# A four-layer convolution sequence: channel mixing on row halves of TensorE, fewer split column transforms, more convolutions put off

## The chip, the cores and the metric

The kernel runs on one core of one Trainium2 chip. The metric is device time in microseconds (us) of one execution. The kernel before takes 2974.68 us, the median of three runs (2972.39 to 2974.85). Engines are named as in the profile: PE is TensorE (PEld its weight loads), DVE is VectorE, ACT is ScalarE, SP is the engine that issues most DMAs.

## The reference, cut to what matters

The input x has 4 images of 64 channels of 256 x 256 float32. Four layers follow one another. Layers 0, 1 and 3 are long convolutions with a separable filter for each channel; layer 2 mixes channels in a Haar transform.

```python
def conv_layer(x, hx, hy, bias):      # layers 0, 1, 3; hx, hy from a small sine network
    k = hx[i, c] * hy[j, c]           # one separable 256 x 256 filter for each channel
    y = irfft2(rfft2(x, 512x512) * rfft2(k, 512x512))[..., :256, :256]
    return y + x * bias[c]            # causal 2D convolution plus a scaled copy

def haar_layer(x, v, conv_w, tau):    # layer 2
    f1 = haar2d(x)
    for i in range(2):
        f4 = einsum('bchw,oc->bohw', f1 * v[i], conv_w[i])
        acc += sign(f4) * relu(abs(f4) - tau[i])
    return haar2d(acc, inverse=True) + x
```

The filter is separable and causal, so a convolution is two products with Toeplitz matrices, one for rows and one for columns. A float32 value enters the matmuls in full precision.

## The kernel before, in words

**Units.** Work goes by image b and channel c. One channel image is a tile of 128 partitions by 2 x 256 (two halves of the rows). A convolution has two stages: `first` contracts the image with the Toeplitz tile of one axis (`contract`, L190 and L191), ACT copies the result out of PSUM (L199); `second` contracts that with the other axis's tile and DVE adds the bias term (L212). A `contract` is two halves m, each of one float32 matmul of 256 columns and one of 128. Toeplitz tiles `t` are read from small padded filters in DRAM (L181).

**`convolutions(b, ...)`** runs layers 0 and 1 on all channels of an image, then the forward Haar transform along the row in three parts: `pairs` (L257, L258), `levels` (L269, L270), and along the column by TensorE in `down`. For a channel in `in_parts`, `split` makes two f32r parts of it: ACT casts it (L280) and DVE subtracts the cast from it (L281). `down` then does two f32r matmuls of 512 columns with the sign matrix (L288). For a channel not in `in_parts`, `down` does a single float32 matmul of 512 columns on the tile itself (L292) and no `split`. Before, all channels of all images are in `in_parts`. ACT copies the coefficients out (L296), and SP stores them to `coef` in DRAM.

**`mixing(b, start, n_act)`** goes over 64 groups g of four coefficient rows. `load` brings a tile `f` in which partitions 0 to 63 hold the 64 channels of two rows and partitions 64 to 127 those of two others (r = 0, 1). `mix` (L335 to L346) multiplies it with `wb`, a block-diagonal matrix of 128 x 256: four matmuls of 256 columns into two PSUM banks. Half of `wb` is zero. Then 16 blocks of 64 values are scaled by v: 16 - `n_act` of them in one DVE instruction (L357), `n_act` by ACT, one instruction each (L359). `shrink` takes magnitude and sign on ACT (L365, L366) and subtracts the threshold on DVE (L367), `signed` multiplies (L372), `add` writes the sum of the two mixings into z in SBUF (L376). `n_act` is 12 for images 0 to 2 and 6 for image 3.

**`inverse(b, start, put_off)`** goes over the 64 channels: `fetch` loads `keep` and copies the channel out of z (L396), `rows` does the inverse transform along the row (L403, L404) and splits the result (L406 on ACT, L407 on DVE), `cols` does the column (L416) and adds the residual (L420, L423, L424). The result u then goes through layer 3 (`last`, two contractions and a store of the output from ACT's queue, L443), except for the channels in `put_off`: their u is stored to `late` in DRAM (L434), also from ACT's queue.

**`convolution(which, ticks)`** does layer 3 later for the channels put off by images 0 to 2: SP loads u back as `v` (L453) and the Toeplitz tile, then `last` follows. Before, every third channel is put off: 21 per image, 63 in all.

**Order of the work.** Each stage is entered with `at(tick, place, run, unit)`, and at the end all events are emitted sorted by tick and place (L500). Each engine and each DMA queue then runs its own instructions in that order. The main loop (L487 to L499) lays them out so: the convolutions of image 0 alone; then for each image b its mixing, beside the convolutions of image b + 1, spread over the mixing's ticks and the inverse stage ahead of it; then its inverse. Beside the mixing of image 3, which has no image after it, the put-off convolutions run. After the end of a mixing (`border`) the last column transforms of the next image are set three ticks apart for each one.

```python
    put_off = range(2, C, 3)
...
        mixing(b, start, 12 if b + 1 < B else 6)
        end = start + groups + 3
        if b + 1 < B:
            ready = convolutions(b + 1, spread(ahead, end + 2), in_parts=range(C), border=end)
```

**Buffers.** Incoming images and `v` share three buffers (tag "in"), Toeplitz tiles five, `f` three, mixing results in PSUM two (of two banks each), results of contractions in PSUM four.

Of the kernel before, what the change touches and what calls it, by code (L numbers as in the profile page):

```python
# [9 lines left out]
F32 = mybir.dt.float32  # L10
# [7 lines left out]
P = 128  # L18
# [19 lines left out]
def conv_seq_kernel(ctx, tc, x, fz, fw, bias, decay, haar, haar_row, factors, vt, taut, wmix, out):  # L38
# [14 lines left out]
    nc = tc.nc  # L53
# [15 lines left out]
    hbr = const.tile([P, P], F32R, name="hbr")  # L69
    hrow = const.tile([P, 2, P], F32, name="hrow")  # L70
    hsinv, ident = hrow[:, 0, :], hrow[:, 1, :]
    wb = const.tile([P, 2, P], F32, name="wb")
    bsb = const.tile([P, 3, C], F32, name="bsb")


    z = zpool.tile([P, 2, S, C], F32, name="z")

    sd = zpool.tile([P, 8, 2, 2, P], F32, name="sd")
    keep = [dram.tile([C, P, 2, 2, P], F32, name=f"keep{b}") for b in range(B)]
# [4 lines left out]

    room = z.rearrange("p h r c -> p (h r c)")
    free = [0]

    def part(n, parts=P):  # L90
# [57 lines left out]
    def constants():  # L148
        signs = part(P)
        nc.sync.dma_start(hbt, haar[0])  # L150
        nc.sync.dma_start(signs, haar[1])
        nc.sync.dma_start(hrow, haar_row)
        nc.vector.memset(wb, 0.0)
        for r in range(2):
            nc.sync.dma_start(wb[r * C : (r + 1) * C, r, :], wmix)
        nc.scalar.copy(hb, signs)
        nc.scalar.copy(hbr, hbt)

# [57 lines left out]

    def butterfly(b):

        d = mx.tile([P, 2, C], F32, name=f"bfly_{b}", tag="mag")
        nc.vector.tensor_sub(d, z[:, :, 0, :], z[:, :, 1, :])  # L220
        nc.vector.tensor_add(z[:, :, 0, :], z[:, :, 0, :], z[:, :, 1, :])
        nc.vector.tensor_copy(z[:, :, 1, :], d)

# [90 lines left out]
    def mixing(b, start, n_act):  # L316

        st = {}

        def load(g):  # L320
            f = mx.tile([P, 2, S], F32, name=f"f_{b}_{g}", tag="f", bufs=3)
            nc.sync.dma_start(f, coef[b].rearrange("k c p w -> (k c) p w")[:, 2 * g : 2 * g + 2])
            st[g] = {"f": f}
            if g % GT == 0:
                t = mx.tile([P, 2, GT, 16], F32, name=f"vt_{b}_{g}", tag="vt")
                nc.sync.dma_start(t, scales[g // GT])
                st["vt", g // GT] = t

        def scale(g, i):
            return st["vt", g // GT][:, i, g % GT, :]  # L330

        def over(g, i, n):
            return scale(g, i)[:, :n].unsqueeze(2).to_broadcast([P, n, C])

        def mix(g):  # L335
            f = st[g]["f"]
            ps = psx.tile([P, 2, 2, S], F32, name=f"px_{b}_{g}", tag="mix")
            for q in range(2):
                for h in range(2):
                    nc.tensor.matmul(  # L340
                        ps[:, h, q, :],
                        f[:, q, h * P : (h + 1) * P],
                        wb.rearrange("p r n -> p (r n)"),
                        start=True,
                        stop=True,
                    )  # L346
            if g == 0:

                one, two = ps[:, :, 0, :P], ps[:, :, 0, P:]
                d = mx.tile([P, 2, P], F32, name=f"d_{b}", tag="mag")  # L350
                nc.vector.tensor_copy(d, two)
                nc.vector.tensor_sub(two, one, d)
                nc.vector.tensor_add(one, one, d)
            f4 = mx.tile([P, 16, C], F32, name=f"f4_{b}_{g}", tag="f4")
            px = ps.rearrange("p h q (r i o) -> p (h q r i) o", r=2, i=2)
            n = 16 - n_act
            nc.vector.tensor_tensor(f4[:, :n], px[:, :n], over(g, 0, n), ALU.mult)  # L357
            for j in range(n, 16):
                nc.scalar.mul(f4[:, j], px[:, j], scale(g, 0)[:, j : j + 1])  # L359
            st[g]["f4"] = f4  # L360

        def shrink(g):
            f4 = st[g]["f4"]
            mag = mx.tile([P, 16, C], F32, name=f"mag_{b}_{g}", tag="mag")
            nc.scalar.activation(mag, f4, AF.Abs)  # L365
            nc.scalar.activation(f4, f4, AF.Sign)  # L366
            nc.vector.tensor_sub(mag, mag, over(g, 1, 16))  # L367
            st[g]["mag"] = mag

        def signed(g):  # L370
            mag = st[g]["mag"]
            nc.vector.scalar_tensor_tensor(mag, mag, 0.0, st[g]["f4"], ALU.max, ALU.mult)  # L372

        def add(g):
            parts = st.pop(g)["mag"].rearrange("p (h r i) o -> p h r i o", h=2, i=2)
            nc.vector.tensor_add(z[:, :, 4 * g : 4 * g + 4, :], parts[:, :, :, 0, :], parts[:, :, :, 1, :])  # L376

        for g in range(S // 4):
            at(start + g - 2, 0, load, g)

            for s, (place, stage) in enumerate([(-2.5, mix), (-3.5, shrink), (-4.1, signed), (-4.2, add)]):
                at(start + g + s, place, stage, g)

    def inverse(b, start, put_off):

        st = {}

        def fetch(c):  # L390
            if c == 0:
                butterfly(b)
            r = mx.tile([P, 2, 2, P], F32, name=f"r_{b}_{c}", tag="f", bufs=3)
            nc.sync.dma_start(r, keep[b][c])
            a = mx.tile([P, 2, 2, P], F32, name=f"zc_{b}_{c}", tag="mag")
            nc.scalar.copy(a, z[:, :, :, c].rearrange("p h (i k) -> p h k i", k=2))  # L396
            st[c] = {"r": r, "z": a}

        def rows(c):
            a = st[c]["z"]  # L400
            ps = psm.tile([P, 2, 2, P], F32, name=f"pw_{b}_{c}", tag="mm")
            for m in range(2):
                nc.tensor.matmul(ps[:, m, 0, :], a[:, 0, m, :], hsinv, start=True, stop=True)  # L403
                nc.tensor.transpose(ps[:, m, 1, :], a[:, 1, m, :], ident)  # L404
            w = mx.tile([P, 2, 2, 2, P], F32R, name=f"w_{b}_{c}", tag="f4")
            nc.scalar.copy(w[:, 0], ps)  # L406
            nc.vector.tensor_tensor(w[:, 1], ps, w[:, 0].bitcast(F32), ALU.subtract)  # L407
            st[c]["w"] = w
            if c not in put_off:
                st[c][2] = toeplitz(2, c, f"t2_{b}_{c}")  # L410

        def cols(c):
            ps = psm.tile([P, 2, 2, P], F32, name=f"pu_{b}_{c}", tag="mm")
            flat = "p m e w -> p (m e w)"
            for i in range(2):
                nc.tensor.matmul(  # L416
                    ps.rearrange(flat), hb, st[c]["w"][:, i].rearrange(flat), start=(i == 0), stop=(i == 1)
                )
            t = io.tile([P, 2, 2, P], F32, name=f"t_{b}_{c}", tag="res", bufs=BUFS["res"])
            nc.vector.scalar_tensor_tensor(t, st[c]["r"], 0.5, ps, ALU.mult, ALU.add)  # L420
            u = io.tile([P, 2, S], F32, name=f"u_{b}_{c}", tag="y", bufs=BUFS["y"])
            v = u.rearrange("p m (w e) -> p m w e", e=2)
            nc.vector.tensor_add(v[:, :, :, 0], t[:, :, 0, :], t[:, :, 1, :])  # L423
            nc.vector.tensor_sub(v[:, :, :, 1], t[:, :, 0, :], t[:, :, 1, :])  # L424
            st[c]["u"] = u

        ends = last(b, st)
        for c in range(C):

            at(start + c, -1, fetch, c)  # L430
            at(start + c + 1, -9, rows, c)
            at(start + c + 2, -8, cols, c)
            if c in put_off:
                at(start + c + 3, -5, lambda c: nc.scalar.dma_start(late[b, c], st.pop(c)["u"]), c)  # L434
            else:
                for s, stage in enumerate(ends):
                    at(start + c + 3 + s, s - 7, stage, c)

    def last(b, st):
        return [  # L440
            first(b, st, "u", 2, "a3"),
            second(b, st, "a3", 2, "u", "y3", "co"),
            lambda c: nc.scalar.dma_start(out[b, c].rearrange("(k p) w -> p k w", p=P), st.pop(c)["y3"]),  # L443
        ]

    def convolution(which, ticks):

        for (b, c), tick in zip(which, ticks):
            st = {}

            def load(c, b=b, st=st):
                u = io.tile([P, 2, S], F32, name=f"v_{b}_{c}", tag="in", bufs=3)
                nc.sync.dma_start(u, late[b, c])  # L453
                st[c] = {"u": u, 2: toeplitz(2, c, f"t2_{b}_{c}")}

            for s, stage in enumerate([load, *last(b, st)]):
                at(tick + s, -s, stage, c)


# [1 line left out]
        return [begin + i * (end - begin - 1) // (n - 1) for i in range(n)]  # L461


    put_off = range(2, C, 3)

    one, two, three = filters(0, nc.scalar), filters(1, nc.scalar), filters(2, nc.sync)

# [17 lines left out]
    ahead = C  # L485
    start = ready + 3
    for b in range(B):  # L487
        mixing(b, start, 12 if b + 1 < B else 6)
        end = start + groups + 3
        if b + 1 < B:  # L490
            ready = convolutions(b + 1, spread(ahead, end + 2), in_parts=range(C), border=end)
        else:
            convolution(
                [(i, c) for i in range(B - 1) for c in sorted(put_off)], spread(start - 2, end + 2, (B - 1) * len(put_off))
# [116 lines left out]
```

## Time and profile before

| What | us |
|---|---|
| Median of 3 runs | 2974.68 |
| The profiled execution | 2975.2 |
| Its span | 2973.4 |
| Matmuls of the mixing (L340), busy | 488.2 |
| Convolutions' matmuls `py<-t,a` (L190), busy | 919.0 |
| DVE threshold L367 and product L372, busy | 312.4 and 311.7 |
| ACT scaling L359, busy | 582.3 |
| ACT casts of the split L280, DVE subtractions L281, busy | 177.6 and 176.1 |
| DMA, mean over the span | 219 GB/s |

The granted TensorE clock is 1.0 throughout. The profile is of one execution; its own time stands 1.8 us above its span. A busy time is the union of an engine's instructions, so instructions that overlap count once. Each engine runs in order, so an instruction that waits holds up all behind it on that engine. The chain of waits gives PE by far the largest share. DVE's busy time is an average over stages with different limits, so each stage has to be looked at alone. Where an f32 matmul is written in the kernel, the trace has two MATMUL and two LDWEIGHTS instructions.

### The profile page before, as it was taken

What the parts mean: (1) busy time and instruction counts of PE and PEld (TensorE: products, weight loads), DVE (VectorE), ACT (ScalarE), POOL (GpSimd) and SP (SyncE); (2) the same over time, 40 slices, a digit from 0 to 9 for tenths busy, and PEclk for the clock granted to TensorE, in tenths of its full rate; (3) what the DMA queues carried; (4) which work ended last, traced back from release to release, by engine and by line L of the source; (5) the groups of instructions that cost most, each with busy time, mean ns of one, the idle gap of its engine ahead of it and who ended that gap; (6) DMA issues with size and microseconds to landing.
All of it is one profiled execution on the core that took longest, in us unless ns stands there. A gap on an engine that the chain in (4) does not pass through costs nothing. (4 is left out here: it accounts for less than half of the span.)

```text
span 2973.4 us, 52066 instructions
## 1 busy us (share of the span) xinstructions
PE 2913.8 (98%) x16950; PEld 2615.1 (88%) x16950; DVE 2545.5 (86%) x4571; ACT 2156.9 (73%) x5014; POOL 0.2 (0%) x4
## 2 busy tenths in 40 slices
PE   8999999999999999999999999999999999999999
PEld 6898988888888898888888988888888988888998
DVE  5766768999998879999989879999998889998776
ACT  2333338999986758889986668989986768887554
POOL 0000000000000000000000000000000000000000
PEclk9999999999999999999999999999999999999999
DMA  5877777666667876776777876777777878777676
GB/s 159 247 237 226 229 228 212 203 202 207 207 196 244 250 217 200 208 216 204 208 219 244 250 225 197 209 210 211 207 216 237 256 236 235 233 230 217 212 212 186
DMA packets 562497, 649.73 MB, mean 219 GB/s; under 512 B 44369, under 2 KB 447412, under 8 KB 562100
## 3 DMA queue, kind: packets, MB, share of 16 engines
q1 hardware_dynamic: 482996, 562.07, 64.8%
q10 hardware_dynamic: 79232, 84.34, 8.0%
q8 instruction: 137, 2.24, 0.3%
q14 instruction: 132, 1.08, 0.1%
HBM read 426.77 MB, written 219.48 MB: 217 GB/s over the span
## 5 line engine op out<-in xcount | busy, mean ns | idle before, releaser
L190 PE MATMUL py<-t,a 128*128 128x256 f32 x3072 | 919.0, 381 | 8.9 <-ACT a L199 5.5
L199 ACT COPY a<-pa 128x512 f32<-128x512 f32 x768 | 477.2, 621 | 387.9 <-PE pa L191 357.2
L359 ACT ACTIVATE f<-px,vt 128x64 f32<-128x64 f32 x2688 | 582.3, 358 | 143.5 <-DVE f L357 143.4
L191 PEld LDWEIGHTS py<-t,a 128*128 128x128 f32 x3072 | 583.4, 190 | 79.3
L191 PE MATMUL py<-t,a 128*128 128x128 f32 x3072 | 590.0, 274 | 0.0
L190 PEld LDWEIGHTS py<-t,a 128*128 128x128 f32 x3072 | 500.4, 191 | 50.9 <-ACT a L199 12.4
L340 PE MATMUL px<-wb,f 128*128 128x256 f32 x2048 | 488.2, 380 | 4.9 <-ACT f L359 4.9
L340 PEld LDWEIGHTS px<-wb,f 128*128 128x128 f32 x2048 | 369.5, 190 | 47.0 <-ACT f L359 6.7
L367 DVE TENSOR_TENSOR mag<-mag,vt 128x1024 f32<-128x1024 f32 x256 | 312.4, 1220 | 28.3 <-ACT mag L365 26.9
L190 PE MATMUL pa<-t,y 128*128 128x256 f32 x1024 | 311.6, 386 | 22.4 <-DVE y L212 20.3
L406 ACT CAST w<-pw 128x512 fp32r<-128x512 f32 x256 | 150.2, 587 | 227.0 <-PE pw L404 218.9
L372 DVE SCALAR_TENSOR_TENSOR mag<-mag,f 128x1024 f32<-128x1024 f32 x256 | 311.7, 1218 | 1.9
L190 PE MATMUL pa<-t,x 128*128 128x256 f32 x1024 | 305.9, 380 | 0.4 <-issue 0.4
L365 ACT ACTIVATE mag<-f 128x1024 f32<-128x1024 f32 x256 | 293.7, 1147 | 11.0 <-DVE z L376 8.8
L366 ACT ACTIVATE f<-f 128x1024 f32<-128x1024 f32 x256 | 285.2, 1114 | 3.0
L396 ACT COPY zc<-z 128x512 f32<-128x512 f32 x256 | 282.0, 1103 | 0.7 <-ACT w L406 0.4
L281 DVE TENSOR_TENSOR sp<-sd,sp 128x512 fp32r<-128x512 f32 x256 | 176.1, 688 | 91.4 <-ACT sp L280 90.2
L190 PE MATMUL pa<-t,u 128*128 128x256 f32 x772 | 232.8, 383 | 2.9 <-PE pu L416 1.6
L420 DVE SCALAR_TENSOR_TENSOR t<-r,pu 128x512 f32<-128x512 f32 x256 | 174.9, 683 | 60.4 <-PE pu L416 57.0
L212 DVE SCALAR_TENSOR_TENSOR y<-x,bsb,py 128x512 f32<-128x512 f32 x256 | 190.1, 742 | 37.9 <-PE py L191 36.1
L212 DVE SCALAR_TENSOR_TENSOR y<-y,bsb,py 128x512 f32<-128x512 f32 x256 | 190.0, 742 | 34.2 <-PE py L191 33.1
L191 PEld LDWEIGHTS pa<-t,x 128*128 128x128 f32 x1024 | 194.6, 190 | 26.3
(67 smaller groups left out, 4458.9 us busy)
## 6 DMA issues: line engine op xcount, KB each, us to landing
t<-pad SPq DMA_DIRECT2D x768, 256.0 KB, 3.9
x<-in_x SPq DMA_DIRECT2D x256, 256.0 KB, 3.6
keep<-sd SPq DMA_DIRECT2D x256, 256.0 KB, 2.9
coef<-co SPq DMA_DIRECT2D x256, 256.0 KB, 3.3
f<-coef SPq DMA_DIRECT2D x256, 256.0 KB, 3.2
r<-keep SPq DMA_DIRECT2D x256, 256.0 KB, 3.3
out_y<-y ACTq DMA_DIRECT2D x256, 256.0 KB, 3.6
late<-u ACTq DMA_DIRECT2D x63, 256.0 KB, 2.9
```

What stands on the lines that cost most here:

```text
L190: nc.tensor.matmul(ps[:, m, :], src[:, 0, m * P : (m + 1) * P], t[:, ::-1], start=True, stop=False)
L191: nc.tensor.matmul(ps[:, m, P:], src[:, 1, m * P : (m + 1) * P], t[:, : P - 1 : -1], start=False, stop=True)
L199: nc.scalar.copy(a, ps)
L212: nc.vector.scalar_tensor_tensor(y, s[res], bsb[:, layer, c : c + 1], ps, ALU.mult, ALU.add)
L281: nc.vector.tensor_tensor(w[:, 1], t, w[:, 0].bitcast(F32), ALU.subtract)
L340: nc.tensor.matmul(ps[:, h, q, :], f[:, q, h * P : (h + 1) * P], wb.rearrange("p r n -> p (r n)"), start=True, stop=True,)
L359: nc.scalar.mul(f4[:, j], px[:, j], scale(g, 0)[:, j : j + 1])
L365: nc.scalar.activation(mag, f4, AF.Abs)
L366: nc.scalar.activation(f4, f4, AF.Sign)
L367: nc.vector.tensor_sub(mag, mag, over(g, 1, 16))
L372: nc.vector.scalar_tensor_tensor(mag, mag, 0.0, st[g]["f4"], ALU.max, ALU.mult)
L396: nc.scalar.copy(a, z[:, :, :, c].rearrange("p h (i k) -> p h k i", k=2))
```

## The change

- `wb` becomes one block of 64 x 128, held twice: on partitions 0 to 63 and on 64 to 127. Its memset goes.
- `mix` does eight matmuls of 64 rows and 128 columns, alternating between the two halves of the rows, in place of four of 128 rows and 256 columns. The results of half r go to PSUM bank r.
- z is laid out by half first (`[P, 2, 2, P, C]`), and the butterfly, the add, the copy in `fetch` and the coefficient tables made on the host follow that order.
- Image 0's column transforms stay split. For image 1 only the last eight channels are split; for images 2 and 3 the even channels and the last eight.
- Put off are the channels with c % 5 in (2, 4): 25 per image, 75 in all.
- The outputs of put-off convolutions are stored from SP's queue; those of the inverse stages stay on ACT's.
- `n_act` in the last mixing goes from 6 to 8.

```diff
-    wb = const.tile([P, 2, P], F32, name="wb")
+    wb = const.tile([P, P], F32, name="wb")
...
-    z = zpool.tile([P, 2, S, C], F32, name="z")
+    z = zpool.tile([P, 2, 2, P, C], F32, name="z")
...
-        nc.vector.memset(wb, 0.0)
         for r in range(2):
-            nc.sync.dma_start(wb[r * C : (r + 1) * C, r, :], wmix)
+            nc.sync.dma_start(wb[r * C : (r + 1) * C], wmix)
...
-            ps = psx.tile([P, 2, 2, S], F32, name=f"px_{b}_{g}", tag="mix")
-            for q in range(2):
-                for h in range(2):
-                    nc.tensor.matmul(
-                        ps[:, h, q, :],
-                        f[:, q, h * P : (h + 1) * P],
-                        wb.rearrange("p r n -> p (r n)"),
-                        start=True,
-                        stop=True,
-                    )
+            ps = psx.tile([P, 2, 2, 2, P], F32, name=f"px_{b}_{g}", tag="mix")
+            for h in range(2):
+                for q in range(2):
+                    for r in range(2):
+                        rows = slice(r * C, (r + 1) * C)
+                        nc.tensor.matmul(
+                            ps[:, r, h, q, :], f[rows, q, h * P : (h + 1) * P], wb[rows], start=True, stop=True
+                        )
...
-            px = ps.rearrange("p h q (r i o) -> p (h q r i) o", r=2, i=2)
+            px = ps.rearrange("p r h q (i o) -> p (r h q i) o", i=2)
...
-            parts = st.pop(g)["mag"].rearrange("p (h r i) o -> p h r i o", h=2, i=2)
-            nc.vector.tensor_add(z[:, :, 4 * g : 4 * g + 4, :], parts[:, :, :, 0, :], parts[:, :, :, 1, :])
+            parts = st.pop(g)["mag"].rearrange("p (s q i) o -> p s q i o", q=2, i=2)
+            rows = z.rearrange("p r h i c -> p (r h) i c")[:, :, 2 * g : 2 * g + 2, :]
+            nc.vector.tensor_add(rows, parts[:, :, :, 0, :], parts[:, :, :, 1, :])
...
-            nc.scalar.copy(a, z[:, :, :, c].rearrange("p h (i k) -> p h k i", k=2))
+            nc.scalar.copy(a, z[:, :, :, :, c].rearrange("p k h i -> p h k i"))
...
-        ends = last(b, st)
+        ends = last(b, st, nc.scalar)
...
-            lambda c: nc.scalar.dma_start(out[b, c].rearrange("(k p) w -> p k w", p=P), st.pop(c)["y3"]),
+            lambda c: queue.dma_start(out[b, c].rearrange("(k p) w -> p k w", p=P), st.pop(c)["y3"]),
...
-            for s, stage in enumerate([load, *last(b, st)]):
+            for s, stage in enumerate([load, *last(b, st, nc.sync)]):
...
-    put_off = range(2, C, 3)
+    put_off = [c for c in range(C) if c % 5 in (2, 4)]
...
-        mixing(b, start, 12 if b + 1 < B else 6)
+        mixing(b, start, 12 if b + 1 < B else 8)
...
-            ready = convolutions(b + 1, spread(ahead, end + 2), in_parts=range(C), border=end)
+            in_parts = [c for c in range(C) if c >= C - 8 or (b > 0 and c % 2 == 0)]
+            ready = convolutions(b + 1, spread(ahead, end + 2), in_parts=in_parts, border=end)
```

## The prediction

> **What bounds the kernel now.** I read the page first, then cut the span into stages, then read each stage's busy times, groups and waits. The page says TensorE:
>
> ```profile
> PE 2913.8 (98%) x16950; PEld 2615.1 (88%) x16950; DVE 2545.5 (86%) x4571; ACT 2156.9 (73%) x5014; POOL 0.2 (0%) x4
> ```
>
> 86% for VectorE is an average. The stages can be cut at the four first mixings (L351) and the four butterflies (L220). This is the busy time by windows from the first mixing on; the columns are length, then busy us of PE, weight loads, DVE, ACT, POOL, the granted clock, the DMA share and GB/s. The rows are mixing 0, inverse 0, mixing 1, inverse 1, mixing 2, inverse 2, mixing 3, inverse 3 (M0, I0, M1 and so on below):
>
> ```profile
> 455.00:866.00 411.00, 401.56 (x2207) 355.35 (x2207) 392.82 (x681) 380.57 (x1093) 0.00 (x0) 1.00 0.68 204
> 866.00:1094.00 228.00, 223.64 (x1401) 200.47 (x1400) 188.26 (x371) 145.66 (x208) 0.00 (x0) 1.00 0.77 236
> 1094.00:1547.00 453.00, 447.27 (x2505) 401.36 (x2505) 422.19 (x739) 397.89 (x1117) 0.00 (x0) 1.00 0.71 207
> 1547.00:1768.00 221.00, 220.03 (x1387) 198.49 (x1386) 183.96 (x368) 144.24 (x206) 0.00 (x0) 1.00 0.79 242
> 1768.00:2221.00 453.00, 447.45 (x2507) 401.58 (x2506) 422.25 (x741) 398.19 (x1118) 0.00 (x0) 1.00 0.71 208
> 2221.00:2438.00 217.00, 215.58 (x1360) 194.30 (x1359) 182.73 (x365) 143.16 (x205) 0.00 (x0) 1.00 0.80 242
> 2438.00:2720.00 282.00, 273.96 (x1480) 243.38 (x1479) 276.42 (x324) 241.91 (x572) 0.00 (x0) 1.00 0.79 232
> 2720.00:2973.00 253.00, 248.73 (x1589) 228.98 (x1588) 176.88 (x327) 141.54 (x195) 0.00 (x0) 1.00 0.67 204
> ```
>
> To be seen: the inverse stages hang on PE alone (220 of 221 us in I1, DVE 184). The mixing stages hang on PE with DVE close behind (447 and 422 of 453), and in M3 DVE is already ahead (276 of 282, PE 274). So what PE gains in a mixing stage is worth something only down to DVE's time there.
>
> The price of a mixing comes from starts, since a matmul's record is longer than its share of the engine (TensorE in time order in M1; start, length):
>
> ```profile
> 700.40 1.89 PE L340 MATMUL px<-wb,f 128*128 128x256 f32 x8
> 702.12 0.59 PE L190 MATMUL pa<-t,x 128*128 128x256 f32 x2
> 702.56 0.38 PE L191 MATMUL pa<-t,x 128*128 128x128 f32 x2
> 702.78 0.60 PE L190 MATMUL pa<-t,x 128*128 128x256 f32 x2
> ```
>
> A mixing takes 702.12 - 700.40 = 1.72 us: four f32 matmuls, each in two instructions, a slot of 0.216 us for 256 columns. A slot for 128 columns is half, 0.108 to 0.11 (L191: 0.22 for two). One contraction (L190 and L191, two halves) is 2 x (0.44 + 0.22) = 1.31 us, a convolution two of them, 2.62 us.
>
> **What the Trainium skill says.** "TensorEngine Tiling (Array Packing)", Tiling Modes, Key Properties: row tiles work independently, with weight loads and matmuls in parallel, but a change of tiling mode drains TensorE. The trace of before shows neither. "TensorE: Matmul & The Clock Gate", Part 3: a weight load overlaps a running matmul of another row group, and matmuls start strictly in program order; nothing here shows it. The same page, LDWEIGHTS: a load's time goes by its columns, not its rows, about columns/1.2 ns, so 107 for 128. The trace fits: in it two weight loads never start less than 108 ns apart. But the matmul slots are no shorter, so it can't say which of the two sets the pace. "Perfetto Trace Analysis", Tensor Engine Instruction: a matmul's start is observed and its end estimated; hence starts above.
>
> **The change, part by part.** The sum is made against the profiled execution: 2975.2 us, of which 2973.4 are span. The median of the runs is 2974.7, so the same figure serves for both.
>
> *Mixing on two row halves (L335-346).* Eight matmuls of 64 rows and 128 columns take the place of four of 128 rows and 256: 16 instructions with 16 weight loads of 128 columns, where 8 and 8 were. Each f32 matmul is two instructions on its own half. They start in order; the second of half 0 must follow the first, the first of half 1 can run beside it, and so on down the chain: 9 slots of 0.108, 0.97 us. The halves r write different PSUM banks, so nothing forbids it. To this come two mode switches. Lower bound for one: 0. Upper: the 0.167 us by which a record exceeds its slot (275 - 108 ns) plus 0.11 for a load that can't be drawn ahead, 0.28. I take 0.05[...]: 1.07 us per mixing. Bounds: 0.86 (8 slots, no switch) and 16 x 0.108 + 0.56 = 2.29 (loads or matmuls take turns). Gain at 1.07: 0.65 x 64 = 42 us of PE in each mixing stage.
>
> *Fewer split column transforms (L278-297).* A split one costs ACT one cast (L280) and DVE one subtraction (L281), and lets PE do two f32r passes of 512 columns:
>
> ```profile
> L280 ACT CAST sp<-sd 128x512 fp32r<-128x512 f32 x52 | 37.9, 728 | 0.2 <-DVE sd L270 0.2
> L288 PE MATMUL pz<-sp,hbr 128*128 128x512 f32 x103 | 36.7, 436 | 0.0
> L281 DVE TENSOR_TENSOR sp<-sd,sp 128x512 fp32r<-128x512 f32 x52 | 35.7, 686 | 2.9 <-ACT sp L280 2.6
> ```
>
> The two passes together take 0.46 us (the like pair at L416, by starts). A whole f32 transform of 512 columns isn't in the trace; from L190's slot it is 2 x 2 x 0.216 = 0.86, so +0.40 on PE each, -0.69 on DVE, -0.73 on ACT. The lines in the trace give 50 transforms to M0 and 52 to M1 and M2, 12 to each inverse. Whole from now on: all 50 in M0, 26 of the 52 in M1 and in M2 (odd channels), and 4, 2, 2 in I0 to I2. Image 0 keeps its splits, so the 455 us ahead of M0 stand.
>
> *Twelve more convolutions put off (25 instead of 21 per image).* Each leaves an inverse stage, 4 x 2.62 = 10.5 us of PE apiece, and enters M3 with all it issues: two contractions, an ACT copy, a DVE add (L212), loads of v and t and a store; the store of u in the inverse stage takes the place of the output's on the same queue.
>
> *M3's split of work (6 to 8 of 16 columns on ACT).* L357 goes from 640 to 512 elements: 817 ns and 420 ns for 256 elements give 685, so -0.132 x 64 = -8.5 us on DVE. ACT gets 128 more L359 at 85.3/384 = 0.22: +28 us.
>
> *The put-off stores from ACT's queue to SP's.* ACT loses the issues of 63 stores of 0.38 us (24 us, not in its busy time) and its waits for y3. On SP the store waits for y3, and behind it are the loads of f, v and t. The loads of v already wait there for the same L212 (77 us in 57 waits in M3), so these come no later. f is asked for two ticks ahead (8.8 us) and lands in 3.2. Cost taken: 0; if that cover is too thin, a bound of 10 us. DMA in M3 rises by 12 x 0.79 MB, from 232 to about 263 GB/s; the busiest 40 us of the inverse stages show 260.
>
> *The layout of z.* The copy L396 (1104 ns, elements 512 bytes apart) reads with half that step. Between no change and the 587 ns of L406, which reads as many contiguous elements: 64 x 0 to 0.5 us off ACT in an inverse stage, where ACT is 65% busy. Nothing, either way. The add L376 and the butterfly keep their counts and sizes. One memset less: off the path.
>
> **The sum.**
> - M0: PE 401.6 - 42 + 20 = 379.4; DVE 392.8 - 34 = 358, ACT 344. PE idled 9.4 before, mostly behind DVE; with DVE relieved I take 6: 385.4, so -25.6.
> - M1, M2: PE 447.3 - 42 + 10.4 = 415.5; DVE 422.2 - 18 = 404, ACT 379. With 6 idle 421.5, so -31.5 each.
> - M3: PE 274 - 42 + 31.4 = 263; DVE 276.4 - 8.5 + 12 x 0.67 (0.74 less the overlap that the union of busy time shows) = 276; ACT 241.9 + 28 + 7 = 277. DVE and ACT are both full: 284, so +2.
> - I0 to I2: -31.4 + 8 x 0.4 = -28.2. PE stays the bound; DVE's share rises by some 4 points. I3 stands.
>
> In all -25.6 - 63 + 2 - 28.2 = -114.8: 2975.2 - 114.8 = 2860 us.
>
> What is late next: in M1 and M2 DVE, 11 us behind PE; in M3 DVE and ACT together.
>
> **The rivals.**
> A, the forecast: 2860, own range 2825 to 2900. Low end: mixing at 0.86 makes M0 371 and leaves M1 and M2 to DVE at 410, together about 2821.
> B, the switches eat most of it. At 1.45 per mixing the gain is 18 us a stage: M0 +2, M1 and M2 -7.5 each, M3 (PE-bound again, 287.5 + 8) +13, inverse -28: 2947. For it: two drains per 4.4 to 7 us tick. Against: PE reads ahead elsewhere.
> C, the other side: no overlap at all, because weight loads share one path and take 0.108 each. At 1.73 PE gains nothing and still pays: M0 +20, M1 and M2 +10.4 each, M3 274 + 31.4 + 8 = 313 (+31), inverse -28: +44, 3019; with both drains at their bound 36 us more per mixing stage, 3160. It decides from 1.56 us per mixing on (2947 and 28 us of gain over 256 mixings). For it: the 108 ns between loads. Against: the loads may be paced by the matmuls.
> D, three full engines hold one another up. If the busiest reaches only 95%, M0 is 399, M1 and M2 437, M3 291: 2912. For it: ACT's 46 us behind L357 in M1. Against: M3 ran at 98% with two full engines.
>
> That the halves aren't addressed as row tiles at all is C.
>
> **The numbers.** A 0.50, D 0.13, B 0.18, C 0.19. Measurement can tell about 0.2% (6 us) from no change. Faster: A, D and nearly all of B, 0.80. Within: 0.02, between B and C. Slower: 0.18, the rest of C. The range takes in A, D and B, 2825 to 2955; C is left out.
>
> **What would show it.** A mixing of about 1.07 us from its first matmul to the next line's, with starts of the two halves in pairs; M1 near 421 with PE and DVE both above 95%; M3 near 284 with ACT above 95%; the inverse stages 9 to 10 us shorter. Wrong if the 16 starts of a mixing stay 0.108 apart one by one (C), if PE stands still at its edges (B), or if PE waits for DVE or ACT for tens of us in M1 (D).

## The result, and the profile after

The changed kernel takes 3052.11 us, the median of four runs (3046.51 to 3058.34), against 2974.76 us before: a ratio of 1.026, with a 95% interval of 1.0235 to 1.0285. It is slower by 77 us where 115 us of gain were forecast. The granted TensorE clock was 0.994 to 0.998 in these four runs and 1.0 before. That is at most 0.6% of the span, 18 us of the 77 by an estimate from these figures; e2 below loses 68 us at a clock of 0.999 to 1.0. The profiled execution has a span of 3044.7 us. The first part of its page, busy time by engine:

```profile
PE 2867.6 (94%) x18998; PEld 2503.2 (82%) x18998; DVE 2487.8 (82%) x4458; ACT 2130.5 (70%) x5030; POOL 0.2 (0%) x4
```

Every engine has less to do than before and all are idle more. The windows by stage, cut at the same events (shown are M0, I0, M1 and I3):

```profile
453.00:887.00 434.00, 394.94 (x2698) 326.69 (x2697) 369.40 (x636) 358.11 (x1037) 0.00 (x0) 1.00 0.64 192
887.00:1110.00 223.00, 216.85 (x1354) 191.84 (x1353) 182.28 (x360) 145.33 (x208) 0.00 (x0) 1.00 0.78 238
1110.00:1577.00 467.00, 435.77 (x2993) 372.71 (x2994) 408.62 (x711) 382.04 (x1090) 0.00 (x0) 1.00 0.67 200
...
2781.00:3044.00 263.00, 257.47 (x1640) 236.72 (x1638) 181.70 (x333) 144.86 (x200) 0.00 (x0) 1.00 0.68 204
```

M1 has become 14 us longer with 12 us less work on PE, 14 less on DVE and 16 less on ACT. No engine is full there: 436, 409 and 382 of 467 us. M3 (not shown) is 304 us instead of 281 with DVE at 278.

The mixing itself does what the change says. TensorE in time order in M0, where L343 is the mixing on halves and L292 a whole column transform:

```profile
700.96 1.02 PE L292 MATMUL pz<-sd,hbt 128*128 128x512 f32 x2
701.82 0.59 PE L189 MATMUL py<-t,a 128*128 128x256 f32 x2
...
704.22 0.38 PE L190 MATMUL pa<-t,y 128*128 128x128 f32 x2
704.53 1.16 PE L343 MATMUL px<-wb,f 64*128 64x128 f32 x16
705.63 0.70 PE L189 MATMUL py<-t,a 128*128 128x256 f32 x2
```

Sixteen instructions take 1.09 us from the first start to the next line's. Their single starts in the trace come in pairs: 7 ns apart within a pair, 112 ns from pair to pair, but 214 ns from the first pair to the second. The start of the first is 205 ns after the instruction ahead of it, where 112 are usual. On the way back, the next line starts 202 ns after the last of the sixteen, which is inside the 1.09, and its second instruction comes 320 ns after its first, where 216 are usual. So a mixing costs 1.09 + 0.09 + 0.10, some 1.29 us, instead of 1.73. That saves 0.44 us, or 28 us in each mixing stage. A whole transform takes 0.86 us, as worked out.

The time is lost in waits. The groups of M1 that grew most (busy us and mean ns, then the idle time ahead of them and what ended it):

```profile
L358 ACT ACTIVATE f<-px,vt 128x64 f32<-128x64 f32 x768 | 167.2, 366 | 80.0 <-DVE f L356 80.0
L366 DVE TENSOR_TENSOR mag<-mag,vt 128x1024 f32<-128x1024 f32 x64 | 78.2, 1222 | 50.4 <-ACT mag L364 50.4
L189 PE MATMUL pa<-t,y 128*128 128x256 f32 x232 | 73.1, 397 | 19.8 <-DVE y L211 19.7
```

Before, these three waits were 46, 11 and 5 us (who waited for whom in M1: us in total, times, longest):

```profile
ACT f L359 <- DVE f L357: 45.9, 45, 2.5
DVE mag L367 <- ACT mag L365: 10.9, 12, 2.8
PE pa L190 <- DVE y L212: 4.9, 7, 1.7
```

ACT waits for DVE, DVE for ACT, and PE for both: a loop.

**The loop.** DVE and ACT in M1 of the kernel before, cut to the instructions of the loop. Call them S (threshold, L367), F (DVE's part of the scaling, L357), G (product, L372); on ACT the twelve scalings L359, then the magnitude L365:

```profile
1298.96 1.22 DVE L367 TENSOR_TENSOR mag<-mag,vt 128x1024 f32<-128x1024 f32 x1
1300.10 0.42 DVE L357 TENSOR_TENSOR f<-px,vt 128x256 f32<-128x256 f32 x1
...
1300.52 1.22 DVE L372 SCALAR_TENSOR_TENSOR mag<-mag,f 128x1024 f32<-128x1024 f32 x1
1300.55 2.56 ACT L359 ACTIVATE f<-px,vt 128x64 f32<-128x64 f32 x12 [0.75 <-DVE f L357]
...
1304.38 1.17 ACT L365 ACTIVATE mag<-f 128x1024 f32<-128x1024 f32 x1
...
1305.90 1.22 DVE L367 TENSOR_TENSOR mag<-mag,vt 128x1024 f32<-128x1024 f32 x1
```

S of group g, then F of g + 1, then ACT's scaling of g + 1, then (after two copies and a cast) its magnitude of g + 1, then S of g + 1: 1.14 + 0.45 + 3.83 + 1.52 = 6.94 us from start to start, about the stage's 453/64 = 7.08 us a group. Steps from start to start add up to the time of a group whatever sets the pace, so the sum alone proves nothing. What speaks for the loop is that most of its steps leave no room: by the medians over M1, F starts before S's record has ended, and ACT's scaling 0.03 us after the end of F. Only S starts 0.36 us after the end of the magnitude, behind other work of DVE. Whether the kernel before was paced by this loop, with PE nearly full beside it, is what e5 to e9 test. In the changed kernel (S is L366, G L371, F L356):

```profile
1312.88 1.22 DVE L366 TENSOR_TENSOR mag<-mag,vt 128x1024 f32<-128x1024 f32 x1
...
1314.21 1.23 DVE L371 SCALAR_TENSOR_TENSOR mag<-mag,f 128x1024 f32<-128x1024 f32 x1
...
1315.35 0.42 DVE L356 TENSOR_TENSOR f<-px,vt 128x256 f32<-128x256 f32 x1
...
1315.80 2.57 ACT L358 ACTIVATE f<-px,vt 128x64 f32<-128x64 f32 x12 [2.37 <-DVE f L356]
```

G now stands between S and F, so the loop is longer by a G, and ACT sits idle for 2.37 us. S now starts 0.03 us after the end of the magnitude (median over M1), so that step leaves no room either. The events sorted by tick and place are not the last word on order, as the description of the kernel before had it. The framework's planner, which lays out the program when it is built, orders each engine's instructions once more: the kernel is written as S of g, F of g + 1, G of g, and the traces show other orders. In M1, G is ahead of F in 12 of 64 groups before and in 36 after; F is ahead even of S, which opens the loop for that group, in 13 before and in 7 after.

### The profile page after: what moved, and what is told of

Same layout as the page of the kernel before. It is cut to its first block, busy times and chain, and to the rows that moved or that the text cites. A ratio compares the mean times of both kernels' runs of the same rounds, so it can differ in the third digit from the quotient of the medians.

```text
span 3044.7 us, 55870 instructions
## 1 busy us (share of the span) xinstructions
PE 2867.6 (94%) x18998; PEld 2503.2 (82%) x18998; DVE 2487.8 (82%) x4458; ACT 2130.5 (70%) x5030; POOL 0.2 (0%) x4
## 3 DMA queue, kind: packets, MB, share of 16 engines
q14 instruction: 131, 1.07, 0.1%
## 4 chain that ended last, share of the span: by engine, by line
PE 27%; DVE 18%; ACT 15%; issue 4%; DMA 4%; SPq 0%; DVEq 0%; ACTq 0%
ACT f L358 8%; PE pa L189 6%; PE py L189 6%; DVE mag L366 4%; ACT mag L364 4%; PE pu L416 3%; PE pw L403 3%; PE pa L190 3%; DVE mag L371 3%; PE py L190 3%; DVE y L211 3%; DVE f L356 2%; DVE sd L269 2%; DVE sd L270 2%; PE pw L404 2%
## 5 line engine op out<-in xcount | busy, mean ns | idle before, releaser
L189 PE MATMUL py<-t,a 128*128 128x256 f32 x3072 | 944.5, 389 | 77.9 <-ACT a L198 72.9
L358 ACT ACTIVATE f<-px,vt 128x64 f32<-128x64 f32 x2816 | 610.9, 354 | 263.1 <-DVE f L356 263.1
L190 PEld LDWEIGHTS py<-t,a 128*128 128x128 f32 x3072 | 584.0, 190 | 79.5
L189 PEld LDWEIGHTS py<-t,a 128*128 128x128 f32 x3072 | 483.4, 191 | 181.1 <-ACT a L198 105.3
L366 DVE TENSOR_TENSOR mag<-mag,vt 128x1024 f32<-128x1024 f32 x256 | 313.0, 1223 | 163.5 <-ACT mag L364 160.4
L371 DVE SCALAR_TENSOR_TENSOR mag<-mag,f 128x1024 f32<-128x1024 f32 x256 | 312.0, 1219 | 3.9 <-ACT f L365 1.7
L343 PE MATMUL px<-wb,f 64*128 64x128 f32 x4096 | 300.2, 285 | 0.0
L396 ACT COPY zc<-z 128x512 f32<-128x512 f32 x256 | 282.4, 1104 | 14.4 <-DVE z L222 6.4
L365 ACT ACTIVATE f<-f 128x1024 f32<-128x1024 f32 x256 | 282.6, 1104 | 4.1
L343 PEld LDWEIGHTS px<-wb,f 64*128 64x128 f32 x4096 | 250.3, 188 | 31.6 <-issue 0.4
L189 PEld LDWEIGHTS pa<-t,y 128*128 128x128 f32 x1024 | 156.6, 192 | 100.3 <-DVE y L211 84.1
L189 PE MATMUL pa<-t,u 128*128 128x256 f32 x724 | 218.7, 384 | 5.2 <-PE pu L416 3.6
L190 PEld LDWEIGHTS pa<-t,y 128*128 128x128 f32 x1024 | 195.4, 191 | 26.8
```

The costliest lines, as they stand in the source:

```text
L189: nc.tensor.matmul(ps[:, m, :], src[:, 0, m * P : (m + 1) * P], t[:, ::-1], start=True, stop=False)
L190: nc.tensor.matmul(ps[:, m, P:], src[:, 1, m * P : (m + 1) * P], t[:, : P - 1 : -1], start=False, stop=True)
L343: nc.tensor.matmul(ps[:, r, h, q, :], f[rows, q, h * P : (h + 1) * P], wb[rows], start=True, stop=True)
L396: nc.scalar.copy(a, z[:, :, :, :, c].rearrange("p k h i -> p h k i"))
```

## The experiments

Theory 1: this loop sets the pace of the mixing stages, and the fewer splits made the planner's order worse. Rival 2: three nearly full engines hold one another up, whatever the order. Rival 3: the row halves cost time themselves.

**One part at a time (e1 to e4).** e1 is the change with its other parts undone, so that the row halves, with the layout of z that goes with them, remain:

```diff
-            in_parts = [c for c in range(C) if c >= C - 8 or (b > 0 and c % 2 == 0)]
+            in_parts = range(C)
-    put_off = [c for c in range(C) if c % 5 in (2, 4)]
+    put_off = range(2, C, 3)
-        mixing(b, start, 12 if b + 1 < B else 8)
+        mixing(b, start, 12 if b + 1 < B else 6)
-            for s, stage in enumerate([load, *last(b, st, nc.sync)]):
+            for s, stage in enumerate([load, *last(b, st, nc.scalar)]):
```

> The kernel before with one part of the change alone: mixing on the two row halves with the new layout of z; all channels split, 21 put off, 6 of 16 columns on ACT, stores from ACT's queue. Theory 1 (the halves work; what was lost came from the order of DVE's and ACT's work, which the planner changed when the splits went): this order stays as before, so M0 about 400, M1 and M2 about 430 each, M3 about 278, in all about 2914 us. Rival 2 (three nearly full engines hold one another up, whatever the order): M1 stays at about 450, in all about 2970. Rival 3 (row halves themselves cost time on or around TensorE): M1 longer than 453, in all above 3000.

Measured: 2994.4 us, ratio 1.0061 (1.0046 to 1.0076); M0 415, M1 458, M3 286. The total is no theory's number; an M1 above 453 is what rival 3 expected. PE is busy for 428 of 458 us in M1, 19 less than before, and none of it came out as time. In the trace of M1, G is ahead of F in 12 groups, as before, but F is ahead of S in 7 instead of 13.

e2 is the kernel before with everything but the halves:

> The kernel before with all of the change but the row halves: fewer splits, 25 put off, 8 of 16 columns on ACT, put-off stores from SP's queue. Theory 1: PE carries the whole column transforms on top of the full mixing and the order flips too, so M1 about 475, M3 about 315, in all about 3055 us. Rival 2 (no matter of order): PE's added work alone, M1 about 464, in all about 3020. Rival 3 (the halves are what costs): below 3000, faster than the changed kernel by 50.

Measured: 3043.5 us, ratio 1.0230 (1.0215 to 1.0246); M1 464, M3 301. The total lies between theory 1 and rival 2, and M1 is rival 2's. Rival 3 is ruled out as the main cause: 68 us are lost without any halves.

e3 undoes the `in_parts` line of the diff above alone, e4 the other three.

> The changed kernel with one part undone: all channels of all images split again. Theory 1: DVE's order in M0 to M2 is as in the kernel before; M1 and M2 about 430 instead of 467 although DVE and ACT do more work, M3 as changed (304), in all about 2920 us. Rival 2: more work on DVE and ACT, M1 470 or more, in all 3050 to 3080. Rival 3: about 3050.

Measured: 3006.0 us, ratio 1.0098 (1.0082 to 1.0115); M1 457, M3 307. Splitting all channels again, which is more work for DVE and ACT, wins 46 us. The direction is theory 1's; its size was 130. The order in the trace of M1 is again that of e1: G is ahead of F in 12 groups and not in 36.

> The changed kernel with another part undone: 21 put off, 6 of 16 columns on ACT in the last mixing, stores from ACT's queue, as before. M0 to M2 as changed (434, 467, 466). Theory 1: M3 back to about 280 and the last inverse to 253, the three earlier inverse stages longer by 9 each, in all about 3043 us. Rival 2 (M3 is long because three engines are full, and the twelve convolutions cost there what they saved): the same within 10. If the put-off part is a gain as forecast: about 3075.

Measured: 3040.0 us, ratio 1.0221 (1.0206 to 1.0237). M3 283 and the last inverse 254, the other three inverse stages longer by 7 each. Theory 1 had 3043. (M3's split between DVE and ACT and the queue of the stores were changed back together with the convolutions put off, so these three aren't told apart.) Together e1, e3 and the changed kernel divide the loss: halves 19 us (e1 less before), the put-off part 12 (e3 less e1), fewer splits 46 (the changed kernel less e3). This holds for this order of steps: on top of everything else the halves lose 9 (the changed kernel less e2).

**DVE's order (e5 to e9).** An edge between two instructions that fixes which comes first, and adds no wait. e5 holds F of the next group ahead of G:

```diff
+        def behind(late, early):
+            tc.add_manual_dep(
+                late.ins, early.ins.name,
+                mybir.DependencyInfo(mybir.DependencyClass.NoSync, mybir.DependencyReason.DATA), reason="order",
+            )
...
-            nc.vector.scalar_tensor_tensor(mag, mag, 0.0, st[g]["f4"], ALU.max, ALU.mult)
+            out4 = nc.vector.scalar_tensor_tensor(mag, mag, 0.0, st[g]["f4"], ALU.max, ALU.mult)
+            if g + 1 in st:
+                behind(out4, st[g + 1]["scaled"])
```

(`st[g]["scaled"]` is F.)

> The changed kernel with one order of work on DVE held fast, by an edge that orders without a wait: the scaling F of group g + 1 ahead of the product G of group g, as it is written. Theory 1 (a loop over two engines sets the pace of the mixing stages: ACT scaling, ACT magnitude, DVE threshold S, DVE scaling F, and again ACT scaling; where the planner puts G between S and F the loop is 1.2 us longer): what the flip cost comes back, M1 and M2 about 455, M0 about 417, in all about 3010 us. Rival 2 (three nearly full engines hold one another up, whatever DVE's order): within 10 us of the changed kernel, 3042 or more. Rival 3 (row halves themselves cost): the same as rival 2.

Measured: 3007.5 us, ratio 1.0109 (1.0092 to 1.0125); M1 455, M0 427. The total and M1 are theory 1's numbers (M0 was to be 417), and nothing but an order was changed. Rivals 2 and 3 expected 3042 or more. Other work of DVE still stands between S and F here: F starts 1.2 us after the end of S (median over M1).

e6 goes further: F of group g + 1 ahead of S of group g, in place of the edge of e5.

```diff
+            scaled = nc.vector.tensor_tensor(f4[:, :n], px[:, :n], over(g, 0, n), ALU.mult)
+            if g > 0:
+                behind(st[g - 1]["sub"], scaled)
```

(`st[g]["sub"]` is S.)

> The changed kernel with F of group g + 1 held ahead of S of group g on DVE, so that ACT's scaling of a group no longer waits for DVE's work on the group before it. Theory 1: the loop is broken, M1 and M2 425 to 435, M0 about 395, M3 about 287, in all about 2920 us. Rival 2: 3030 or more. Rival 3: 3030 or more.

Measured: 2936.3 us, ratio 0.9874 (0.9859 to 0.9889); M0 405, M1 440, M2 438, M3 289. The direction is theory 1's again, and 16 us of its size are missing. The change, slower by 2.6%, is 1.3% faster than the kernel before with one edge per group. M1 by windows:

```profile
1081.00:1521.00 440.00, 428.45 (x2997) 369.89 (x2996) 408.86 (x710) 382.88 (x1090) 0.00 (x0) 1.00 0.70 212
```

In e6 the scaling on ACT (L366 here) can start while S (L374) runs:

```profile
1295.35 0.42 DVE L362 TENSOR_TENSOR f<-px,vt 128x256 f32<-128x256 f32 x1 [0.27 <-PE px L349]
1295.69 1.22 DVE L374 TENSOR_TENSOR mag<-mag,vt 128x1024 f32<-128x1024 f32 x1
1295.81 2.57 ACT L366 ACTIVATE f<-px,vt 128x64 f32<-128x64 f32 x12 [0.55 <-DVE f L362]
```

F now waits for PE's result, where it waited behind S. The same edge on e1 and on the kernel before:

> Row halves alone (all channels split, 21 put off) with the same order, F of group g + 1 ahead of S of group g. Theory 1: with the loop broken what PE saves shows: M1 and M2 about 432 (DVE is then the bound, 422 busy), M0 about 400, in all about 2922 us. Rival 2: about 2990, as without the order. Rival 3: no faster than the kernel before under the same order.

Measured: 2939.0 us, ratio 0.9883 (0.9868 to 0.9897); M1 441, with DVE busy for 423 of it and PE for 426. 2922 and 432 were expected; no engine is full, and what holds the rest is open.

> The kernel before with the same order, F of group g + 1 ahead of S of group g. Theory 1: PE, at 448 busy of 453 in M1, is next after the loop, so little is won: M1 about 451, in all 2960 to 2975 us. Rival 2: within 5 us of the kernel before. If the order alone wins as much here as it does with the halves, PE was no bound at all and the halves are worth nothing.

Measured: 2954.6 us, ratio 0.9931 (0.9916 to 0.9946); M1 447, PE busy for 446. More than expected was won: M1 came down by 6 us, to where PE is full. So the loop was the limit before, and PE stood next, 6 us behind it. With the loop broken the halves are worth 16 us (e7 less e8); without that they were worth less than nothing (e1).

e9 is the flip alone, in the kernel before, with F held behind G in M0 to M2:

> The kernel before with nothing changed but DVE's order in M0 to M2: F of group g + 1 held behind G of group g in every group, the flip that the planner made in 30 groups of M1 in the changed kernel (and in 12 in the kernel before). Theory 1 (the loop through F): M1 from 453 to 470 or more, M0 to 430, in all 3020 to 3060 us. Rival 2 (order doesn't matter, engines are full): within 10 us of the kernel before.

Measured: 3085.4 us, ratio 1.0361 (1.0345 to 1.0376); M0 468, M1 481. M1 by windows:

```profile
1146.00:1628.00 482.00, 463.28 (x2522) 407.53 (x2521) 425.91 (x740) 399.45 (x1117) 0.00 (x0) 0.99 0.67 196
```

No instruction was added or taken away; the order costs 3.6%, more than expected. G is ahead of F in 63 groups of each stage, where it was in 3, 12 and 12. (The expectation's 30 groups for the changed kernel are 36 in the trace.) The granted clock was 0.990 in the profiled execution against 1.0 before, which is at most some 30 of the 108 us, by an estimate of 1% of the span.

**What is left once the order is mended (e10, e11, e15).** All three have the edge of e6. e10 is e6 with M3's part as before (what e4 undid), e11 is e10 with more splits, and e15 is e11 with M3's part as changed. The line for more splits:

```diff
-            in_parts = [c for c in range(C) if c >= C - 8 or (b > 0 and c % 2 == 0)]
+            in_parts = [c for c in range(C) if c >= C - 8 or (c % 2 == 0 if b == 0 else c % 4 != 1)]
```

> The changed kernel with F of group g + 1 ahead of S of group g, and with 21 put off, 6 of 16 columns on ACT in the last mixing and stores from ACT's queue, as before. Theory 1: M0 to M2 as with that order in the changed kernel (405, 439, 438), M3 and the last inverse as before (281, 253), the other inverse stages longer by 7 each: about 2930 us, so the put-off part costs 5 to 10 us rather than winning 26. If the put-off part is a gain once the order is mended: 2945 or more.

Measured: 2946.5 us, ratio 0.9899 (0.9882 to 0.9915); M0 404, M1 438, M3 280. The stages came as expected; they add up to 2946, and the 2930 was a wrong sum. By the expectation's own test (2945 or more) the put-off part is a gain here: e6, which has it, is 10 us lower, or 7 by the ratios to the runs beside each. The two intervals just overlap, so this isn't certain.

> As the one before it, but with more channels split: every even channel of image 1, three in four of images 2 and 3 (and the last eight of each). With the loop broken PE should be the bound of the mixing stages again (428 busy of 439 in M1, DVE 409), and every split takes 0.4 us off PE: M0 about 399, M1 and M2 about 435, in all about 2918 us. If PE isn't the bound: no gain, 2930.

Measured: 2935.8 us, ratio 0.9859 (0.9844 to 0.9874); M0 403, M1 435. It is 11 us below e10, which ran beside it, where 12 were expected. In the profiles M0 and I0 together are 9 us shorter, M1 and M2 2.6 and 2.1. DVE and ACT have more to do in e11 than in e10, so neither was the limit; PE, busy for 426 of 435 us in M1, is nearest to it.

> The changed kernel with F of group g + 1 ahead of S of group g, more channels split (every even channel of image 1, three in four of images 2 and 3, and the last eight of each), its put-off part kept: M0 to M2 as in the tuned run (403, 435, 435), M3 and the inverse stages as with the order alone in the changed kernel (289, 260; 221, 219, 214). About 2931 us; if the put-off part is worth something under this order it is below the tuned run, which had the old one.

Measured: 2937.3 us, ratio 0.9864 (0.9851 to 0.9878); M3 292, last inverse 260, the other inverse stages 213, 221, 218. About 2931 were expected. Against e11 nothing is won or lost: with these splits the put-off part is worth nothing, where e6 against e10 gave 7 to 10 us. e6, e11 and e15 lie within 1.5 us of one another, too near to be told apart.

**Do the halves run side by side because they alternate (e12)?** As e7, with the loop over r outside the loops over h and q.

> Row halves alone with F ahead of S, but all eight instructions of half 0 ahead of all eight of half 1, so that neighbours are on the same half. If it is the alternation that lets two run side by side, a mixing takes 15 to 16 slots, 1.7 to 1.8 us with its switches instead of 1.19, and M1 is 450 or more, in all about 2965 us. If the halves run side by side in any order: about 2939, as with the alternation.

Measured: 2975.3 us, ratio 0.9993 (0.9985 to 1.0002), 36 us above e7; M1 454. The mixing in the trace:

```profile
1304.20 1.71 PE L349 MATMUL px<-wb,f 64*128 64x128 f32 x16
1305.84 0.48 PE L189 MATMUL py<-t,a 128*128 128x256 f32 x1
```

It takes 1.64 us from start to start instead of 1.09. With the same edges on both sides (205 and 320 ns in the trace) that is 1.84 us, 0.11 more than the whole-row mixing of before; 64 times that is the 7 us by which M1 is longer than in e8. So most of the overlap rests on alternation. It is not all or nothing: three pairs of the sixteen starts still lie 4 to 6 ns apart, although all of half 0 stands ahead of half 1 in the program. The first matmul of half 1, known by its longer record (373 ns, like the first of half 0), starts 6 ns after the fifth of half 0. So across the halves the starts don't strictly follow program order, which the prediction took from the page that it names; here the measurement decides.

**Why did e1 lose 19 us (e13, e14)?** The order of DVE and ACT was exchanged between the kernel before and e1, instruction by instruction, with a chain of the same edges (`line` is the other kernel's order):

```diff
+        for early, late in zip(line, line[1:]):
+            tc.add_manual_dep(
+                late, early.name,
+                mybir.DependencyInfo(mybir.DependencyClass.NoSync, mybir.DependencyReason.DATA), reason="order",
+            )
```

> Row halves alone, with DVE's and ACT's instructions held, one by one, in the order that they have in the kernel before. Only TensorE's mixing is then different. Theory 1 (what the planner did to the order is what made row halves alone slower): the 19 us over the kernel before go, M1 at or a little below 453, in all 2955 to 2975 us. Rival 3 (the halves themselves cost, by their switches of mode): still 2985 or more.

Measured: 2984.3 us, ratio 1.0022 (1.0013 to 1.0031). In between, within 1 us of rival 3's 2985.

> The other way round: the kernel before with DVE's and ACT's instructions held in the order that the planner gave to row halves alone. Theory 1: the order costs by itself, 2990 us or more. Rival 3: 2975, as before.

Measured: 2986.9 us, ratio 1.0030 (1.0019 to 1.0042). In between as well, nearer to theory 1's 2990. The order alone costs 10 us here, and the halves alone 7 in e13, of the 19 that e1 lost. So about half of e1's loss is the order, with two reservations. Half of what e14 loses lies in I1 and I2 (4 and 2 us), not in the mixing stages. And e1 ran at a granted clock of 0.996 to 0.997, e13 and e14 at 0.999 to 1.0, which may be part of it. M0, M1 and M3 of e13, cut by windows:

```profile
455.90:866.00 410.10, 379.17 (x2706) 328.95 (x2707) 391.55 (x678) 379.87 (x1092) 0.00 (x0) 1.00 0.68 204
1094.00:1553.00 459.00, 426.82 (x3017) 373.45 (x3014) 421.96 (x741) 398.46 (x1119) 0.00 (x0) 1.00 0.71 206
2446.00:2728.00 282.00, 245.46 (x1983) 213.09 (x1982) 276.10 (x324) 241.35 (x572) 0.00 (x0) 1.00 0.80 232
```

DVE and ACT do the same work in the same order as before, PE is busy 20 to 28 us less in each stage, and M0 and M3 are as long as before, to 0.7 us. What PE saved turned into waits: PE's wait for DVE's y in M1 went from 5 to 29 us. Why M1 is even 5 us longer is open; the order of TensorE's and SP's instructions was not held.

## Why the prediction was wrong, point by point

- **What bounds the kernel.** Here it failed. "The mixing stages hang on PE with DVE close behind" was read from busy shares, 447 and 422 of 453 us, and from it followed that what PE gains is time won down to DVE's. PE was nearly full beside a loop over DVE and ACT that is 6 us a stage longer (e8). The trace had a sign of it: ACT's 46 us behind L357 in M1, which the prediction used only as a point for rival D. e13 shows it: 20 us off PE in M1 and no time won.
- **The sum for M0, M1 and M2.** "PE idled 9.4 before, mostly behind DVE; with DVE relieved I take 6" (the step that turned busy time into length) had no ground. The length was to be 385, 421.5 and 421.5; it was 434, 467 and 467. With the loop broken (e6) it is 405, 440 and 438, still 20, 18 and 17 above. (The 379.4 and 415.5 of its sum are 0.2 low; nothing hangs on it.)
- **Fewer splits.** The number of whole transforms and the 0.40 us on PE, by starts, were right. The savings were smaller than forecast: in M0 23 us of 34 on DVE and 22 of 37 on ACT, in M1 14 of 18 and 16 of 19. What was left out is that the planner orders the work anew for a changed program, and fewer splits lost 46 us. An order was taken as given by the ticks. e5, which holds F ahead of G, takes back 45; it is not quite the same thing, since it also undoes the 12 groups of M1 in which G was ahead before.
- **Mixing on halves.** The overlap was right, and rival C with it wrong. C's 3019 comes nearest to the measured time by chance. The size was off: 1.29 us instead of 1.07. The halves start together, so there are 8 slots and not 9. But a change from whole rows to halves or back costs about 0.2 us (0.09 to the next start and 0.10 to the one after it), where 0.05 was taken: 0.39 for both instead of 0.10. So the term of the sum is 28 us a stage and not 42, and these 14 us are most of what M0 to M2 of e6 lie above the forecast.
- **Put-off convolutions.** Inverse stages 0 to 2 win 22 us (e3 against e1, both with all channels split) where 31 were forecast. In the changed kernel they are only 10 us shorter than before, since whole transforms cost 8 there (e4 less e1) and not 3. As to the rest, M3 was to lose 2 us and lost 21, and the last inverse lost 11, which was not in the sum at all. There, 51 more TensorE instructions (1640 against 1589) are 3.2 of the put-off convolutions at 16 each: the work that doesn't fit in M3 runs on into a stage that PE bounds, 8.4 us at 2.62 each. M3's busy times came near the sum (DVE 278 for 276, ACT 269 for 277, PE 266 for 263), but even with the order mended M3 is 289 and not 284.
- **Stores on SP's queue, the layout of z, the memset.** No cost seen, as forecast: in M3 no wait on a store beyond 2.2 us in all (DVE's y behind a store of the output), and L396 takes 1104 ns as before.
- **The rivals.** D named the right place, ACT behind L357, but as a share that full engines don't reach (2912 us); the loop and its order give a time above the kernel before. Once the order is held, something like D remains: PE, the busiest engine, is busy for 97% of M1 in e6 and in e7, and no run shows what holds it. The forecast's chance for slower, 0.18, was all put on TensorE's loads.

## What to carry to other kernels

Before an engine's busy share is taken for the bound, walk once around the waits between the engines and look for a loop whose steps follow one another without a gap. If there is one, work taken off an engine that stands beside it may win nothing; an edge that breaks the loop tests it, since the sum of the steps can't. When a framework orders instructions, compare the order of the two programs on the engines of that loop; here one product placed ahead of one scaling in each group cost up to 3.6% of the kernel, and one edge per group turned a change that lost 2.6% into one that wins 1.3%. The lowest median is e11's, 2935.8 us: row halves, a few more splits than the change has, and that edge; e6 and e15 are no slower within the spread of the runs.

## What the runs showed of the hardware

- Two f32 matmul instructions of 64 rows and 128 columns on different halves of TensorE's rows start 7 ns apart, and a pair is followed by the next after 112 ns, with a weight load of 128 columns for each of the two. So two such loads, for different halves, fit into a slot of 112 ns. Between loads for whole rows 108 ns stay the least in the trace of before, and which of load and matmul sets that pace stays open.
- Going from whole rows to halves costs 93 ns ahead of the first matmul (205 instead of 112) and 102 more before the second pair (214 instead of 112). Going back costs about 90 ns ahead of the first matmul (202 instead of 112) and 104 more before the second (320 instead of 216).
- With all of half 0 ahead of half 1 the sixteen take 1.64 us instead of 1.09: most of the overlap needs instructions that alternate. The two halves still overlap a little, the first start of half 1 coming 6 ns after the fifth of half 0.
- ACT's copy of 512 elements takes 1104 ns at a step of 512 bytes and 1104 ns at 256.
